# Selective scan: a second of four states by ScalarE products, chunks prepared one chunk earlier, D·x moved into the convolution

## The chip, the cores and the metric

One Trainium2 chip, one core. The metric is the device time of one launch in microseconds (us); lower is better. Engines: PE (TensorE), DVE (VectorE), ACT (ScalarE), POOL (GpSimd), and SP, which here only issues DMAs.

## The reference

Two layers on an image of 256 x 256 tokens with 128 channels, in fp32, each added to its input after a group norm. Layer 0 is a gated attention along rows; the change does not touch it. Layer 1 widens to 256 channels, convolves 3 x 3, and scans the 65,536 tokens in four directions k (row order, column order, and both reversed), with 16 states for each channel:

```
xi, z = split(x @ w_in.T);  z = silu(z);  xc = silu(depthwise_conv3x3(xi))
for each direction k (xs = xc in that order):
    dts, B, C = split(x_proj[k] @ xs)            # 8 + 16 + 16 rows
    delta = softplus(dt_w[k] @ dts + dt_b[k])
    h[t] = exp(delta[t] * A[k]) * h[t-1] + delta[t] * xs[t] * B[t]     # per channel and state
    y_k[t] = sum over states (h[t] * C[t]) + D[k] * xs[t]
out = x + (layernorm(sum_k y_k) * z) @ w_out.T
```

The sum over directions makes the D term of a token (sum of D[k]) * xc.

## The kernel before, in words

Stages one after the other: group norm, attention, convolution (lines 437 to 629), scan (635 to 1173). The convolution goes by blocks of 8 rows, in an order written out by hand: `convolve` (PE), `back` (turns the result to token rows on PE, copies on DVE, and stores xc with one DMA at line 593), `project` (next block; its z goes out by DMA from `zt`, two buffers).

The scan does the directions in the order 2, 1, 3, 0. Each has 128 chunks of T = 512 tokens: 512 chunks q. Of a chunk, the 256 channels are 8 groups g of 32; partition 32j+c of a group holds channel c and, in the free dimension, the states 4j to 4j+3 (i = 0 to 3). So a group is four scans of 128 x 512, and a chunk 32 of them, which I number by slots m = 4g + n, n being the place of the scan in the group's order. The lines:

- `times_B` (875): DVE makes bx[:, :NB] = B_r * ur, for NB = 3 of the four states. B_r holds the rows of B, spread to all partitions by DMA (779); ur is delta*x spread to the group's partitions by a PE product (864). bx has 8 buffers.
- `products` (834), `turn_back` (846): for the fourth state, ACT multiplies delta*x, transposed to token partitions (duT, made by `turn`), by the column of B, 128 columns (four groups) at a time, 32 products a chunk; PE turns the result back by four 128 x 128 transposes a group into bl (PSUM, one buffer).
- The scans (1148): DVE, h = dA*h + bx, in place. dA = exp(delta*A) comes from ACT (1122), into PSUM (three buffers) or, for the state that reads bl, into SBUF (dAl, two buffers). It reads dr, delta spread by DMA (856).
- 1167, 1168: POOL keeps the last column and multiplies the four states by C_r (2048 columns).
- `sums` (890): PE adds up the 16 states with the matrix gather, for four groups (half a chunk) into yp: 32 instructions, emitted in one go at slot 4 of the next chunk and at slot 24. `evacuate` copies yp out on ACT.
- `store` (three directions) adds the running sum yl, loaded by DMA (907), on PE (913, 918), copies it on ACT (940) and stores it; `finish` (the last direction) does the same, then the norm, times z, w_out and the residual.
- `begin_sums` (1073): in the first direction PE starts yp with a product of xs and dg, the diagonal of the summed D.
- `prepare` (721 to 804): from the loaded tokens xs, B, C, delta and du = delta*xs. Softplus is written as max(v,0) + log(1+exp(-|v|)) with a first-order correction: Abs, Relu, Exp, Identity, Identity, Ln on ACT and four POOL operations of 128 x 1024.

The order of all engines' work in the scan is the program's (`manual_schedule`). The loop at line 1103 goes through slots; in each it emits dA, then one piece of each generator that is due (`turning`, `later`, `preparing`, `multiplying`), then the scan, then at fixed n times_B (n = 1), turn_back and spread_du (n = 3). A table `counts` says how many products a slot takes. Engines wait for each other by semaphores, each doing its own list in order. Preparing chunk q+2 begins at slot 21 of chunk q and ends in chunk q+1.

Of the kernel before, what the change touches and what calls it, by code (L numbers as in the profile page):

```python
# [8 lines left out]
F32 = mybir.dt.float32  # L9
# [57 lines left out]
def attention_and_scan_kernel(  # L67
# [35 lines left out]
    y_d = {k: dram.tile([NT, DI], F32, name=f"y{k}_d") for k in (1, 2, 3)}  # L103
# [333 lines left out]
    with tc.tile_pool(name="cw", bufs=1) as cw, tc.tile_pool(name="cs", bufs=2) as cs:  # L437
# [31 lines left out]

        cps = tc.tile_pool(name="cps", bufs=2, space=PSUM)  # L470
# [107 lines left out]
        def back(k, h, xct, xcs):  # L578
# [12 lines left out]
            if h == 1:  # L591
                t0 = RB * k * S
                nc.sync.dma_start(
                    xc_d[t0 : t0 + RB * S, :].rearrange("(c j p) d -> p c j d", p=P, c=4), xct
                )

# [40 lines left out]
    NB = 3  # L637
# [17 lines left out]
    D_s = sw.tile([P, K, 2], F32, name="D_s")  # L655
    nc.scalar.dma_start(D_s, Ds)
    for k in range(1, K):
        nc.vector.tensor_add(D_s[:, 0], D_s[:, 0], D_s[:, k])
    dg = sw.tile([P, 2, P], F32, name="dg")
    for h in range(2):  # L660
        nc.vector.tensor_scalar(dg[:, h, :], ident, D_s[:, 0, h : h + 1], None, ALU.mult)
# [18 lines left out]
    neg_one = sw.tile([P, 1], F32, name="neg_one")  # L680
    nc.vector.memset(neg_one, -1.0)
# [23 lines left out]
    loaded, prepared, summed, turned, products_of = {}, {}, {}, {}, {}  # L705

    def load(q):
        k, a = steps[q]
        xt = io.tile([P, 4, DI], F32, name="xtok", bufs=1)
        src = tokens(xc_d, k, a)  # L710
        n = 4 // len(src)
        for w, s in enumerate(src):
            nc.sync.dma_start(xt[:, n * w : n * w + n, :], s)
        loaded[q] = xt
# [6 lines left out]
    def prepare(q):  # L721
# [13 lines left out]
        yield from until(2, 5)  # L735
# [8 lines left out]
        yield  # L744
        yield
# [4 lines left out]
        yield  # L750


        e = io.tile([P, 2, T], F32, name="e", bufs=1)
        delta = io.tile([P, 2, T], F32, name="delta", bufs=1)
        pvs = []
        for h in range(2):
# [4 lines left out]
            pvs.append(pv)  # L761
        yield
        yield
        for h, pv in enumerate(pvs):
            nc.scalar.activation(e[:, h, :], pv, AF.Abs, bias=dtb_s[:, k, h : h + 1])  # L765
            nc.scalar.activation(delta[:, h, :], pv, AF.Relu, bias=dtb_s[:, k, h : h + 1])
            yield
# [5 lines left out]
        nc.scalar.activation(e, e, AF.Exp, scale=-1.0)  # L773
        B_r = io.tile([P, NB, T], F32, name="B_r")
        C_r = io.tile([P, NI, T], F32, name="C_r")
        for m, t, ni in ((0, B_r, NB), (1, C_r, NI)):
# [6 lines left out]
        yield  # L783
        lg = io.tile([P, 2, T], F32, name="lg", bufs=1)
        nc.scalar.activation(lg, e, AF.Identity, bias=1.0)
        yield
        du = io.tile([P, 2, T], F32, name="du")
        nc.scalar.activation(du, lg, AF.Identity, bias=neg_one)
        B_t = io.tile([P, 4, R + 2 * NS], F32, name="B_t")
        nc.scalar.copy(B_t, tp)  # L790
        yield
        nc.gpsimd.tensor_tensor(e, e, du, ALU.subtract)  # L792
        yield
        yield
        nc.scalar.activation(lg, lg, AF.Ln)  # L795
        yield
        nc.gpsimd.tensor_tensor(lg, lg, e, ALU.add)  # L797
        yield
        nc.gpsimd.tensor_tensor(delta, delta, lg, ALU.add)  # L799
        de_d = sd.tile([DI, T], F32, name="de_d")  # L800
        nc.sync.dma_start(de_d.rearrange("(h p) t -> p h t", p=P), delta)
        yield
        nc.gpsimd.tensor_tensor(du, delta, xs, ALU.mult)  # L803
        prepared[q] = xs, de_d, du, B_r, C_r, B_t

    def turn(q):

        duT = io.tile([P, 4, DI], F32, name="duT", bufs=1)
        turned[q] = duT
        tps = []  # L810
        for w in range(2):
            tp = sps.tile([P, 2, DI], F32, name="tpd", tag="mm")
            for b in range(2):
                for h in range(2):
                    t0 = (2 * w + b) * P
                    nc.tensor.transpose(
                        tp[:, b, h * P : (h + 1) * P], prepared[q][2][:, h, t0 : t0 + P], ident
                    )
            tps.append(tp)
        yield  # L820
        for w, tp in enumerate(tps):
            nc.scalar.copy(duT[:, 2 * w : 2 * w + 2, :], tp)
            yield

    def products(q, h):


        bt = wk.tile([P, 4, 4, 4, 32], F32, name=f"bt{h}", bufs=1)
        products_of[q, h] = bt
        duT, B_t = turned[q], prepared[q][5]  # L830
        for b in range(4):
            for j in range(4):
                n = R + NI * j + NB
                nc.scalar.mul(  # L834
                    bt[:, b, :, j, :],
                    duT[:, b, h * P : (h + 1) * P].rearrange("t (g c) -> t g c", c=32),
                    B_t[:, b, n : n + 1],
                )
                yield

    def turn_back(q, g):

        bl = sps.tile([P, T], F32, name="bl", bufs=1)
        bt = products_of[q, g // 4]
        for b in range(4):
            nc.tensor.transpose(  # L846
                bl[:, b * P : (b + 1) * P], bt[:, b, g % 4].rearrange("t j c -> t (j c)"), ident
            )
        return bl

    def spread_delta(q, h):

        de_d = prepared[q][1]
        dr = io.tile([P, 4, T], F32, name="dr")
        for j in range(4):
            nc.sync.dma_start(
                dr[32 * j : 32 * j + 32],
                de_d[h * P : (h + 1) * P, :].rearrange("(q c) t -> c q t", c=32),
            )
        return dr  # L860

    def spread_du(q, g):
# [4 lines left out]
            prepared[q][2][:, g // 4, :],  # L867
# [5 lines left out]
    def times_B(q, ur):  # L873
        bx = wk.tile([P, NI, T], F32, name="bx", bufs=8)
        nc.vector.tensor_tensor(  # L875
            bx[:, :NB, :],
            prepared[q][3],
# [5 lines left out]
    def sums(q, h):  # L883
# [4 lines left out]
        for i in range(NI):  # L888
            for g, hc in enumerate(his):
# [4 lines left out]
                    start=(i == 0 and steps[q][0] != ORDER[0]),  # L894
# [5 lines left out]
    def load_sum(q):  # L900
# [3 lines left out]
        src = tokens(y_d[ORDER[ORDER.index(k) - 1]], k, a)  # L904
# [5 lines left out]
    def add_sum(ps, yl, blocks):  # L910

        if yl is not None:
            nc.tensor.matmul(ps, ident, yl, start=True, stop=True, skip_group_check=True)  # L913
        for o, yo in blocks:
            if yl is None:
                nc.tensor.transpose(o, yo, ident)
            else:
                nc.tensor.matmul(o, yo, ident, start=False, stop=True, skip_group_check=True)

    def store(q, yos):  # L920
# [3 lines left out]
        yl = summed.pop(q, None)  # L924
        yield
        tps = []
        for h, yo in enumerate(yos):
# [4 lines left out]
                None if yl is None else yl[:, :, hs_],  # L932
# [14 lines left out]
    def finish(q, yos):  # L947
# [25 lines left out]
        zt = io.tile([P, 2, T], F32, name="zl", bufs=1)  # L973
        nc.sync.dma_start(zt, z_d[:, a : a + T].rearrange("(h p) t -> p h t", p=P))
# [11 lines left out]
        yield from until(6, 15)  # L986
        yn = io.tile([P, 4, DI], F32, name="yn", tag="yl", bufs=1)
        for j, now, then in ((0, 15, 16), (1, 16, 19), (2, 19, 20), (3, 20, 27)):
# [7 lines left out]
            yield from until(now, then)  # L996
# [8 lines left out]
        yield from until(27, 31)  # L1005
        gz = io.tile([P, 2, T], F32, name="gz", bufs=1)
# [5 lines left out]
        yield from until(33, 36)  # L1012
# [221 lines left out]
```

## Time and profile before

| what | value |
|---|---|
| median of 3 timed runs (lowest, highest) | 32187.19 us (32186.76, 32198.17) |
| profiled execution, first to last instruction | 32185.1 us, mean PE clock 0.853 |
| busy: PE, DVE, ACT, POOL | 23853.4, 29575.2, 25201.0, 25710.4 us |
| L1148 scans, fed from PSUM dA, from dAl | 12192 at 1264 ns, 4064 at 1254 ns |
| L875 product with B, 128 x 1536 | 4096 at 1727 ns |
| L1122 exp into PSUM, into SBUF | 12288 at 683 ns, 4096 at 713 ns |
| L834 products, 128 x 128 | 16384 at 392 ns |
| L1168 product with C, 128 x 2048 | 4096 at 4542 ns |
| ACT table loads in the scan | 2 a chunk, 1283 ns each |

"L875" is line 875 of the kernel. A row such as `bx<-B_r,ur 128x1536 ... x4096` names what is written and read, the shape and the count. A mean can be longer than the distance from start to start, since instructions of an engine overlap by some 0.1 us. Where the order of time is shown, the columns are start (us), duration (us), engine, line, operation, and in brackets the idle time before it and who ended it.

### The profile page before, as it was taken

The numbers are of one execution on the slowest core, as the hardware profiler recorded it, in microseconds if no ns is written. First come the engines' busy times: TensorE is split into PE (matmuls) and PEld (weight loads), VectorE is DVE, ScalarE is ACT, GpSimd is POOL, SyncE is SP. The second block draws the span as 40 slices with busy tenths as digits, with TensorE's granted clock in tenths as the row PEclk, the third lists the DMA queues.
The fourth block names the chain that finished last, engine by engine and source line by source line (L and its number), as shares of the span: only waits on it lengthen the run. The fifth ranks groups of instructions, "written<-read, shape, count | busy, mean of one in ns | idle before, by whom it ended". The sixth has DMA issues, their size and how long they took to land.

```text
span 32185.1 us, 380702 instructions
## 1 busy us (share of the span) xinstructions
PE 23853.4 (74%) x122902; PEld 10868.3 (34%) x122902; DVE 29575.2 (92%) x29023; ACT 25201.0 (78%) x50438; POOL 25710.4 (80%) x11291
## 2 busy tenths in 40 slices
PE   6999988666676667777777777777777777777777
PEld 3555544222222222222222232223222333333333
DVE  7666633999999999999999999999999999999999
ACT  5555522888888888888888888888888888888888
POOL 4222200999999999999999999999999999999998
PEclk9999999888888888888888888888888888888888
DMA  4001033444444444444444444444444555555554
GB/s 143 30 28 29 27 105 121 110 109 108 111 109 108 110 110 118 119 121 120 119 120 122 119 119 121 121 119 119 122 119 118 123 124 124 123 123 123 124 123 113
DMA packets 2100469, 3518.55 MB, mean 109 GB/s; under 512 B 201112, under 2 KB 1187096, under 8 KB 2022560
## 3 DMA queue, kind: packets, MB, share of 16 engines
q1 hardware_dynamic: 2093296, 3476.09, 43.3%
q8 instruction: 967, 15.84, 0.2%
q10 hardware_dynamic: 5168, 18.12, 0.1%
q14 instruction: 1038, 8.50, 0.1%
HBM read 2754.18 MB, written 739.25 MB: 109 GB/s over the span
## 4 chain that ended last, share of the span: by engine, by line
PE 32%; ACT 24%; DVE 22%; issue 12%; POOL 9%; DMA 2%; SPq 0%; ACTq 0%; POOLq 0%; DVEq 0%
DVE bx L1148 11%; PE yp L890 8%; DVE bx L875 7%; ACT dA L1122 6%; PE ur L864 6%; POOL bx L1168 5%; PE pb L741 3%; ACT bt L834 2%; PE pc L563 2%; ACT dAl L1122 2%; PE av L393 2%; PE tpy L913 2%; POOL at L370 2%; ACT e L765 2%; ACT L795 2%
## 5 line engine op out<-in xcount | busy, mean ns | idle before, releaser
L1168 POOL TENSOR_TENSOR bx<-bx,C_r 128x2048 f32<-128x2048 f32 x4096 | 18604.4, 4542 | 334.3 <-POOL hst L1167 5.8
L1148 DVE TENSOR_TENSOR_SCAN bx<-dA,hst,bx 128x512 f32<-128x512 f32 x12192 | 15074.4, 1264 | 217.2 <-ACT dA L1122 215.3
L1122 ACT ACTIVATE dA<-dr,A_s 128x512 f32<-128x512 f32 x12288 | 8329.3, 683 | 2247.5 <-DVE bx L1148 2199.6
L864 PE MATMUL ur<-du,spread 128*128 128x512 f32 x8192 | 5710.1, 787 | 4498.5 <-DVE bx L875 4378.8
L875 DVE TENSOR_TENSOR bx<-B_r,ur 128x1536 f32<-128x1536 f32 x4096 | 7075.5, 1727 | 40.1 <-DMA dr<-de_d 40.1
L834 ACT ACTIVATE bt<-duT,B_t 128x128 f32<-128x128 f32 x16384 | 5572.5, 392 | 698.7 <-PE bl L846 698.7
L1148 DVE TENSOR_TENSOR_SCAN bx<-dAl,hst,bl 128x512 f32<-128x512 f32 x4064 | 5096.6, 1254 | 24.2 <-PE bl L846 24.1
L890 PE MATMUL yp<-bx,gather 128*32 128x512 f32 x32768 | 5052.5, 771 | 7.5 <-POOL bx L1168 6.4
L846 PE MATMUL bl<-ident,bt 128*128 128x128 f32 x16384 | 2714.8, 289 | 2441.0 <-DVE bx L1148 2439.0
L846 PEld LDWEIGHTS bl<-ident,bt 128*128 128x128 f32 x16384 | 1791.0, 143 | 4323.4 <-DVE bx L1148 3240.7
L864 PEld LDWEIGHTS ur<-du,spread 128*128 128x128 f32 x8192 | 1451.2, 223 | 5027.9 <-DVE bx L875 5023.9
L370 POOL TENSOR_TENSOR at<-at,sm 128x2048 f32<-128x2048 f32 x256 | 922.2, 3603 | 2719.7 <-DVE sm L369 2550.6
L1122 ACT ACTIVATE dAl<-dr,A_s 128x512 f32<-128x512 f32 x4096 | 2919.2, 713 | 0.0
L890 PEld LDWEIGHTS yp<-bx,gather 128*32 128x32 f32 x32768 | 1165.1, 139 | 4348.3 <-issue 3834.9
L1167 POOL COPY hst<-bx 128x4 f32<-128x4 f32 x4096 | 771.4, 188 | 1615.5 <-DVE bx L1148 1588.6
L362 ACT ACTIVATE at<-at,mx 128x256 f32<-128x256 f32 x2048 | 1016.1, 498 | 472.5 <-DVE mx L358 468.1
L792 POOL TENSOR_TENSOR e<-e,du 128x1024 f32<-128x1024 f32 x512 | 1202.8, 2349 | 138.3 <-DMA C_r<-bc_d 138.3
L799 POOL TENSOR_TENSOR delta<-delta,lg 128x1024 f32<-128x1024 f32 x512 | 1209.9, 2363 | 40.1
L803 POOL TENSOR_TENSOR du<-delta,xs 128x1024 f32<-128x1024 f32 x512 | 1205.4, 2354 | 40.2
L758 PE MATMUL pv<-bc,dtw_s 8*128 8x512 f32 x2048 | 1019.6, 616 | 256.5 <-ACT bc L747 256.5
L797 POOL TENSOR_TENSOR lg<-lg,e 128x1024 f32<-128x1024 f32 x512 | 1205.0, 2354 | 0.2 <-ACT lg L795 0.2
L391 DVE COPY aT<-atp 128x512 f32<-128x512 f32 x512 | 353.6, 691 | 774.8 <-PE atp L382 771.0
(173 smaller groups left out, 31933.7 us busy)
## 6 DMA issues: line engine op xcount, KB each, us to landing
dr<-de_d SPq DMA_DIRECT2D x4096, 256.0 KB
C_r<-bc_d SPq DMA_DIRECT2D x2048, 256.0 KB
B_r<-bc_d SPq DMA_DIRECT2D x2048, 192.0 KB
de_d<-delta SPq DMA_DIRECT2D x512, 512.0 KB
xtok<-xc_d SPq DMA_DIRECT2D x256, 512.0 KB
xtok<-xc_d SPq DMA_DIRECT2D x512, 256.0 KB
yl<-y_d SPq DMA_DIRECT2D x512, 256.0 KB
y_d<-yt SPq DMA_DIRECT2D x512, 256.0 KB
```

Of the source, the lines that this page charges most:

```text
L370: nc.gpsimd.tensor_tensor(at, at, sm.unsqueeze(3).to_broadcast([P, H, 2, S]), ALU.mult,)
L797: nc.gpsimd.tensor_tensor(lg, lg, e, ALU.add)
L799: nc.gpsimd.tensor_tensor(delta, delta, lg, ALU.add)
L803: nc.gpsimd.tensor_tensor(du, delta, xs, ALU.mult)
L834: nc.scalar.mul(bt[:, b, :, j, :], duT[:, b, h * P : (h + 1) * P].rearrange("t (g c) -> t g c", c=32), B_t[:, b, n : n + 1],)
L846: nc.tensor.transpose(bl[:, b * P : (b + 1) * P], bt[:, b, g % 4].rearrange("t j c -> t (j c)"), ident)
L864: nc.tensor.matmul(ur, spread[:, g % 4].rearrange("p j c -> p (j c)"), prepared[q][2][:, g // 4, :], start=True, stop=True,)
L875: nc.vector.tensor_tensor(bx[:, :NB, :], prepared[q][3], ur.unsqueeze(1).to_broadcast([P, NB, T]), ALU.mult,)
L890: nc.tensor.matmul(yp[32 * g : 32 * g + 32, :], gather, hc[:, i, :], start=(i == 0 and steps[q][0] != ORDER[0]), stop=True, skip_group_che ...
L1122: nc.scalar.activation(dA, dr, AF.Exp, scale=A_s[:, k, g // 4, g % 4, i : i + 1])
L1148: nc.vector.tensor_tensor_scan(hs[:, i, :], dA, hs[:, i, :] if i < NB else bls.pop((q, g)), 0.0 if a == 0 else hst[:, g, i : i + 1], ALU.mult,
L1168: nc.gpsimd.tensor_tensor(hs, hs, prepared[q][4], ALU.mult)
```

## The change

- NB goes from 3 to 2: two states of four come by ACT products. A product now takes all 8 groups, 256 columns; there are still 32 a chunk, one in every slot, into bt2 and bt3 with two buffers each, made a whole chunk ahead. turn_back runs twice a group, at n = 1 and n = 3, into bl2 and bl3 (one PSUM buffer each). The order of states in a group is 2, 0, 3, 1. dA in PSUM has two buffers instead of three.
- bx has 7 buffers instead of 8.
- `prepare(q+2)` starts at slot 6 of chunk q and ends in the same chunk, with duT in it; delta is one Softplus activation for each half; du overwrites xs. B_r and C_r of chunk q+1 are loaded from slot 10 of chunk q on (`replicate`).
- dr is loaded by group, two groups ahead, with three buffers.
- `sums` goes out in quarters, one a slot: slots 5 to 8 (for the chunk before) and 21 to 24. `store` and `finish` start at slot 20 and have new distances between their pieces.
- D*xc is made in the convolution on POOL from the block that is stored, and stored to its own array by a DMA; the first direction loads it as its running sum, as the others load theirs. begin_sums loses its product.

The diff, cut:

```diff
-    y_d = {k: dram.tile([NT, DI], F32, name=f"y{k}_d") for k in (1, 2, 3)}
+    y_d = {k: dram.tile([NT, DI], F32, name=f"y{k}_d") for k in (1, 2, 3, K)}
...
+                xd = cs.tile([P, 4, 4, DI], F32, name="xd", bufs=1)
+                nc.gpsimd.tensor_tensor(
+                    xd.rearrange("p c j d -> p (c j) d"),
+                    xct.rearrange("p c j d -> p (c j) d"),
+                    D_row.unsqueeze(1).to_broadcast([P, 16, DI]),
+                    ALU.mult,
+                )
+                nc.sync.dma_start(
+                    y_d[K][t0 : t0 + RB * S, :].rearrange("(c j p) d -> p c j d", p=P, c=4), xd
                 )
...
-    NB = 3
+    NB = 2
...
+        for h, pv in enumerate(pvs):
+            nc.scalar.activation(
+                delta[:, h, :], pv, AF.Softplus, bias=dtb_s[:, k, h : h + 1]
+            )
+        de_d = sd.tile([DI, T], F32, name="de_d", bufs=3)
+        nc.sync.dma_start(de_d.rearrange("(h p) t -> p h t", p=P), delta)
         yield
...
+        nc.gpsimd.tensor_tensor(xs, delta, xs, ALU.mult)
...
+    def products(q):
+        duT, B_t = prepared[q][2], prepared[q][4]
+        products_of[q] = []
+        for i in range(NB, NI):
+            bt = wk.tile([P, 4, NG, 4, 32], F32, name=f"bt{i}")
+            products_of[q].append(bt)
+            for b in range(4):
+                for j in range(4):
+                    n = R + NI * j + i
+                    nc.scalar.mul(
+                        bt[:, b, :, j, :],
+                        duT[:, b, :].rearrange("t (g c) -> t g c", c=32),
+                        B_t[:, b, n : n + 1],
+                    )
+                    yield
+
+    def turn_back(q, g, i):
+        bl = sps.tile([P, T], F32, name=f"bl{i}", bufs=1)
+        bt = products_of[q][i]
...
+    def spread_delta(q, g):
+        dr = io.tile([P, T], F32, name="dr", bufs=3)
+        nc.sync.dma_start(
+            dr, prepared[q][1][32 * g : 32 * g + 32, :].unsqueeze(0).to_broadcast([4, 32, T])
+        )
...
-        bx = wk.tile([P, NI, T], F32, name="bx", bufs=8)
+        bx = wk.tile([P, NI, T], F32, name="bx", bufs=7)
...
+        zt = io.tile([P, 2, T], F32, name="zl", tag="yl", bufs=1)
+        nc.sync.dma_start(zt, z_d[:, a : a + T].rearrange("(h p) t -> p h t", p=P))
...
-        for n, i in enumerate((NB, *range(NB))):
+        for n, i in enumerate((NB, 0, NB + 1, 1)):
             if i < NB:
-                dA = sps.tile([P, T], F32, name="dA", bufs=3)
+                dA = sps.tile([P, T], F32, name="dA", bufs=2)
...
+            if n == 0 and g == 0 and q + 1 < NQ:
+                multiplying.append(products(q + 1))
+            if n == 1 and g == 0 and q + 2 < NQ:
+                load(q + 2)
+            if n == 2 and g == 1 and q + 2 < NQ:
+                preparing.append(prepare(q + 2))
+            if n == 2 and g == 2 and q + 1 < NQ:
+                replicating.append(replicate(q + 1))
...
+            if n == 1 and g == 1 and q:
+                summing.append(sums(q - 1, 1))
+            if n == 1 and g == 5:
+                summing.append(sums(q, 0))
+            if n == 0 and g == 5 and finishing:
+                later.append(finishing.pop())
             pieces(later)
             piece(preparing)
-            for _ in range(counts[g][n] if g in counts else 0):
-                piece(multiplying)
+            piece(replicating)
+            piece(multiplying)
+            piece(summing)
...
             if n == 1 and nxt:
                 bxs[nxt] = times_B(nxt[0], urs.pop(nxt))
-            if n == 3 and nxt:
-                bls[nxt] = turn_back(*nxt)
+            if n % 2 and nxt:
+                bls[(*nxt, n // 2)] = turn_back(*nxt, n // 2)
             if n == 3 and s + 2 < len(all_steps):
                 urs[all_steps[s + 2]] = spread_du(*all_steps[s + 2])
```

## The prediction

> **What bounds the kernel now.** I read the page's slices first, then busy time by stage, then the order of time on VectorE (DVE) and TensorE (PE) inside one chunk. The stages (PE, PE weight loads, DVE, ScalarE/ACT, GpSimd/POOL, then clock, DMA share):
>
> ```profile
> 4200.00:5400.00 1200.00, 1143.47 (x18383) 599.52 (x18381) 387.49 (x565) 272.06 (x453) 17.85 (x42) 1.00 0.37 123
> 12180.00:18660.00 6480.00, 4613.65 (x20266) 1900.17 (x20264) 6454.34 (x5066) 5497.97 (x10636) 5933.89 (x2532) 0.83 0.49 120
> 25340.00:32100.00 6760.00, 4966.00 (x23308) 2389.93 (x23306) 6598.11 (x6020) 5879.15 (x11405) 6375.07 (x3134) 0.83 0.51 123
> ```
>
> The scan runs from 5590 us to the end, 512 chunks. In it DVE is busy 6454 of 6480 us (99.6%), and in the last direction 97.6%: DVE is the bound. One group of a chunk on DVE, in order of time:
>
> ```profile
> 15003.25 1.72 DVE L875 TENSOR_TENSOR bx<-B_r,ur 128x1536 f32<-128x1536 f32 x1
> 15004.89 2.45 DVE L1148 TENSOR_TENSOR_SCAN bx<-dA,hst,bx 128x512 f32<-128x512 f32 x2
> 15007.26 1.25 DVE L1148 TENSOR_TENSOR_SCAN bx<-dAl,hst,bl 128x512 f32<-128x512 f32 x1
> 15008.43 1.25 DVE L1148 TENSOR_TENSOR_SCAN bx<-dA,hst,bx 128x512 f32<-128x512 f32 x1
> 15009.61 1.72 DVE L875 TENSOR_TENSOR bx<-B_r,ur 128x1536 f32<-128x1536 f32 x1
> ```
>
> Start to start, a scan takes 1.175 us, the product with B 1.64, a group 6.36; eight are 50.9, and chunks follow every 51.2 us. PE in the same chunk:
>
> ```profile
> 15011.39 1.71 PE L864 MATMUL ur<-du,spread 128*128 128x512 f32 x2 [2.16 <-DVE bx L875]
> 15013.03 4.70 PE L890 MATMUL yp<-bx,gather 128*32 128x512 f32 x32
> 15017.65 0.66 PE L846 MATMUL bl<-ident,bt 128*128 128x128 f32 x4
> 15018.15 1.02 PE L864 MATMUL ur<-du,spread 128*128 128x512 f32 x2
> 15024.42 2.08 PE L864 MATMUL ur<-du,spread 128*128 128x512 f32 x2 [2.48 <-DVE bx L875]
> 15026.86 2.05 PE L913 MATMUL tpy<-yl,ident 128*128 128x512 f32 x2 [0.36 <-DMA yl<-y_d]
> ```
>
> See two things. PE waits for DVE, often over 2 us, so its bursts (4.70 us of yp) are covered. And the same ur takes 1.02 us in a busy stretch, about 2.0 after a wait: the clock records say 0.5 or 1.0, 0.83 on average.
>
> **What the Trainium skill says.** "ScalarE: Activation LUTs", section "What ACT_TABLE_LOAD costs": 0.833 ns a column, pointer operands extra, and 1283 ns for a table load. The trace agrees: bt at 128 columns 392 ns, dAl at 512 columns 713, loads 1283. "TensorE: Matmul & The Clock Gate", Part 1: an activity monitor halves the clock in free windows of 3.4 us. The trace agrees: its clock records come in multiples of 3.413 us. Matched with PE's busy share in the scan stage, a window under 0.39 was nearly always followed by half clock; full clock held from 0.43 up, and half clock ended only after 0.8 or more. Same page, Part 2: matmuls keep program order; the order of time above shows it.
>
> **The change, part by part.** Slot m = 4g+n of a chunk, T(m) the end of its scan.
>
> *DVE.* The product falls from 1536 to 1024 columns. L401 (512 columns, 692 ns) and L875 (1536, 1727 ns) give 1.01 ns a column, so 0.52 us off 1.64. A group is 5.84, a chunk 46.7 instead of 50.9. That is 4096 x 0.52 = 2130 us, if DVE stays the bound. Both kinds of scan cost the same (1264 and 1254 ns).
>
> *ACT.* Busy now 5498/6480 x 51.2 = 43.4 us a chunk. 32 products at 256 instead of 128 columns add 32 x 0.107 = 3.4 (estimate from the ScalarE page's slope; the trace's bt to dAl slope is 0.836). Abs, Relu, Exp, two Identity, Ln go (4 x 0.57 + 0.95 + 0.95 + 1.04 + 1.06 = 6.3 start to start), two Softplus come: no row and no page shows one, the ScalarE page finds functions equal per column, so I take the Abs price, 0.57 each; the ends are no table load (2.6 us less than now) and four loads (2.6 more). I keep two. Net -1.5: 41.9 of 46.7, still covered. The Softplus burst (2 x 1.28 + 2 x 0.57 = 3.7) lies under four slots of lead, 5.8 us.
>
> *POOL* loses three of four 2.36 us operations, 46.9 to 39.8 us a chunk. *DMA* loses a third of B_r and gains 512 KB a chunk in the first direction: even. dr becomes eight issues, each three buffers ahead, a window of two groups, 11.7 us: covered; on SP it stands behind bc_d, de_d and y_d stores, which wait for ACT work that ACT does anyway before it frees the dr buffer. Loading and preparing a whole chunk earlier moves their DMAs (xtok, bc_d, B_r, C_r, de_d) on SP, with free buffers when they come up: cost 0. In the last direction zl now shares yl's buffer and waits on SP until PE has done tpz; dr for slot 12 stands behind it, about 2 us late of 11.7: 0.
>
> *D·x* in the convolution: two L1168 prices a block, 32 x 9.1 = 290 us on a POOL busy 18 of 1200 us, plus 64 MB written at DMA share 0.37. PE bounds that stage. SP queues z_d stores and the next row loads behind the 9 us wait; zt has two buffers and a pair of units every 20 us. Cost 0; exposed 290. Start-up: chunk 1 is prepared ahead of the first scan and 32 products precede it, +30 us (estimate from the 54 us it takes now).
>
> *PE, where the stall comes from.* bl doubles: 8 more groups at 0.5 us, 36.4 to about 40 us of a shorter chunk; the dg product of the first direction goes, an L913 pair comes in its place. The order matters more. turn_back at slot 19 waits for T(18), since bl3 has one buffer, and all of the following queues behind it: bl3 0.6, ur 1.0, tpy 1.75 (L913 0.86, L918 0.89), sums 0.9 (a quarter of yp at full clock, 8 instructions), bl2 0.6, tpy 1.75, sums 0.9, sums 0.9, bl3 0.6, ur 1.0, sums 0.9, gaps and hand-over 0.3: done at T(18)+11.2. The last sums piece (slot 24) frees the bx buffer that times_B at slot 25 needs, because 7 buffers put group 7 on group 0's. DVE gets there after 7 scans and a product, T(18)+9.3. Stall 1.9 at full clock. Before, 8 buffers and sums drained at group 6 left a whole group of room. Same figure at slots 3 to 9: bl3, ur, four sums, two tps, bl2, bl3, ur end at T(2)+8.45 against 9.3: 0.9 to spare.
>
> Half clock: in light groups PE does bl2, then bl3 and ur, so most windows lie under 0.4 and the clock halves; it returns after one window filled by the burst, 3 to 6.6 us in. That makes the first part (bl3, ur, L913: 2.5 us) about 4.9: +2.35. At slot 5 two to three light groups precede: always, stall 2.35-0.9 = 1.4. At slot 19 about 8 in 10 window positions, shorter: +1.4. With yl landing late and small rest 0.3: 1.9+1.4+1.4+0.3 = 5.0 us a chunk, against 4.2 gained and 0.3 to 1.4 of present stalls removed. ACT and POOL are ahead by then.
>
> Sum: first scan 5590 + 30; 512 x 46.72 = 23,921; norm statistics 128 x 1.57 = 201; stalls 512 x 5.0 = 2560; tail 51: **32,353, say 32,350**. The same sum for before gives 5590 + 26,051 + 201 + 298 (stalls 0.3, and 1.4 in the last direction) + 51 = 32,191 against a span of 32,185.1; the median of the timed runs is 32,187.2.
>
> **Rivals.**
> (B) *The light groups keep the full clock, and only queue length costs.* For: more PE work in every group, a second bl shortens idle stretches. Against: windows holding one bl are still 20% busy. Stall 1.9 + 0.2: 29,793 + 512 x 2.15 = 30,900. It decides if the stall is under 4.6 us a chunk: this is the rival on the faster side.
> (C) *The PE backlog compounds:* tpy waits for yl (issue to landing about 10 us, issued behind ACT's slot 15), the yt copies then hold ACT at slot 25, dA comes late. For: L913 shows waits on the yl DMA already. Against: 14.7 us in total now. 7.0 us a chunk: 33,380.
> (D) Softplus or D·x doesn't do what it says: bounded above at 2.6 us a chunk less and 290 us more; within the range.
>
> **Chances.** My forecast 0.50 (its own range 32,000 to 32,700), B 0.28, C 0.22. Range 30,800 to 33,400. About 0.2% is what a measurement here can tell from no change (32,121 to 32,249). Of my forecast a quarter lies below that and 0.13 within: faster 0.28 + 0.12 = 0.40, same 0.07, slower 0.53.
>
> **What would show it.** Right: the product at 1.1 us start to start; DVE idle before the product with B at groups 2 and 6, released by PE yp; chunks every 51 to 52 us; PE's clock still near 0.83; ACT idle mostly on PE or DVE. B: clock over 0.93 in the scan, chunks near 49. C: DVE waits on ACT dA after yt. Wrong altogether: DVE idle before scans for bl or dr, or POOL releasing yp last.

## The result, and the profile after

The changed kernel takes **32188.24 us** (median of 12 runs, 32177.96 to 32199.31), the kernel before on the same chip 32186.88 us (12 runs). The ratio is 1.000, with a 95% interval of 0.9992 to 1.0009: no difference. I had forecast 32,350 us, slower by 0.5%; the time lies in the range, but the direction that I gave the most chance did not come.

The profiled execution spans 32186.4 us, against 32185.1 before. The same three stages, with the same columns as above (length; PE, PE weight loads, DVE, ACT, POOL; clock, DMA share, GB/s):

```profile
4200.00:5400.00 1200.00, 1149.96 (x18543) 611.23 (x18513) 388.72 (x566) 272.87 (x454) 258.89 (x68) 0.99 0.51 171
12180.00:18660.00 6480.00, 5115.82 (x24291) 2437.91 (x24292) 5916.36 (x5056) 5360.75 (x9863) 5058.63 (x2150) 0.83 0.44 115
25340.00:32100.00 6760.00, 5419.43 (x27443) 2818.91 (x27436) 6132.07 (x6053) 5657.34 (x10693) 5543.45 (x2772) 0.87 0.44 119
```

In the scan DVE falls from 6454 to 5916 us of 6480, so 538 us of work have gone from this stretch, and yet as many instructions (5056 after, 5066 before) pass in it. DVE now stands idle for 8.7% of it. The clock is 0.83, as before. Who ends that idle time is in the view of waits by engine (in all, times, longest, all in us but the times):

```profile
DVE bx L872 <- PE yp L887: 2165.4, 913, 3.8
...
DVE bx L1129 <- ACT dA L1101: 102.4, 196, 4.4
```

913 waits in 512 chunks are nearly two a chunk; L872 is times_B, L887 the sums. In the order of time on DVE, around the longer of the two (slots 23 to 26, then the other wait, at slot 9 of the next chunk):

```profile
15012.42 1.25 DVE L1129 TENSOR_TENSOR_SCAN bx<-dAl,hst,bl 128x512 f32<-128x512 f32 x1
15013.59 1.26 DVE L1129 TENSOR_TENSOR_SCAN bx<-dA,hst,bx 128x512 f32<-128x512 f32 x1
15018.18 1.22 DVE L872 TENSOR_TENSOR bx<-B_r,ur 128x1024 f32<-128x1024 f32 x1 [3.34 <-PE yp L887]
15019.32 1.27 DVE L1129 TENSOR_TENSOR_SCAN bx<-dAl,hst,bl 128x512 f32<-128x512 f32 x1
...
15042.64 1.22 DVE L872 TENSOR_TENSOR bx<-B_r,ur 128x1024 f32<-128x1024 f32 x1 [1.05 <-PE yp L887]
```

And what PE was doing meanwhile:

```profile
15005.65 1.09 PE L846 MATMUL bl<-ident,bt 128*128 128x128 f32 x4 [1.60 <-DVE bx L1129]
15006.53 1.92 PE L861 MATMUL ur<-xs,spread 128*128 128x512 f32 x2
15008.23 1.34 PE L909 MATMUL tpy<-yl,ident 128*128 128x512 f32 x2
15009.41 1.05 PE L911 MATMUL tpy<-ident,yo 128*128 128x128 f32 x8
15010.39 1.07 PE L887 MATMUL yp<-bx,gather 128*32 128x512 f32 x8
15011.39 0.66 PE L846 MATMUL bl<-ident,bt 128*128 128x128 f32 x4
15011.88 1.02 PE L909 MATMUL tpy<-yl,ident 128*128 128x512 f32 x2
15012.74 1.05 PE L911 MATMUL tpy<-ident,yo 128*128 128x128 f32 x8
15013.73 1.92 PE L887 MATMUL yp<-bx,gather 128*32 128x512 f32 x16
15015.58 0.66 PE L846 MATMUL bl<-ident,bt 128*128 128x128 f32 x4
15016.07 1.02 PE L861 MATMUL ur<-xs,spread 128*128 128x512 f32 x2
15017.03 1.07 PE L887 MATMUL yp<-bx,gather 128*32 128x512 f32 x8
```

PE waits for a scan, starts bl3, and then works without a gap for 12.4 us. The first ur takes 1.92 us and the later one 1.02: the burst starts at half clock. Its last quarter of the sums ends at 15018.1, and DVE, which stopped at 15014.8, starts the product at 15018.18. This is the queue that the prediction laid out, in its order.

Summed by group (from one product with B to the next, mean of a direction, worked out from the trace; work is 5.82 us a group):

| | before | after, first direction | after, last direction |
|---|---|---|---|
| plain group | 6.36 | 5.82 | 5.82 |
| group 2 (slot 9) | 6.67 | 7.00 | 5.97 |
| group 6 (slot 25) | 6.36 | 9.26 | 10.42 |
| chunk | 51.20 | 51.26 | 53.60 |

In the first three directions after, each chunk has 1.17 us of wait at slot 9 and 3.43 at slot 25: 4.6 us, against 4.3 saved on eight products. These are means; most chunks take 51.20 us, as before, and some take more. In the last direction the waits come to 5.4 us, with 1.57 us of norm statistics in group 7. The chunks before took 51.20, 51.19, 51.18 and 53.88 us by direction.

### The profile page after: what moved, and what is told of

Its sections match the earlier page's. It is cut to its first block, busy times and chain, and to the rows that moved or that the text cites. A ratio compares the mean times of both kernels' runs of the same rounds, so it can differ in the third digit from the quotient of the medians.

```text
span 32186.4 us, 417546 instructions
## 1 busy us (share of the span) xinstructions
PE 25927.0 (81%) x140314; PEld 13062.6 (41%) x140314; DVE 27464.9 (85%) x29024; ACT 24568.8 (76%) x47363; POOL 22480.8 (70%) x9787
## 4 chain that ended last, share of the span: by engine, by line
PE 49%; DVE 29%; issue 10%; ACT 5%; DMA 3%; POOL 3%; SPq 0%; POOLq 0%; ACTq 0%; DVEq 0%
DVE bx L1129 18%; PE yp L887 13%; PE ur L861 9%; PE bl L846 8%; DVE bx L872 7%; DMA yl<-y_d 2%; PE tpy L909 2%; PE tpy L911 2%; PE pc L575 2%; PE av L393 2%; POOL at L370 2%; ACT bt L834 2%; PE atp L382 2%; PE tps L743 1%; DVE at L357 1%
## 5 line engine op out<-in xcount | busy, mean ns | idle before, releaser
L846 PE MATMUL bl<-ident,bt 128*128 128x128 f32 x32768 | 6314.9, 324 | 5392.8 <-DVE bx L1129 5392.1
L1129 DVE TENSOR_TENSOR_SCAN bx<-dAl,hst,bl 128x512 f32<-128x512 f32 x8128 | 10276.7, 1264 | 121.6 <-ACT dA L1101 78.3
L1129 DVE TENSOR_TENSOR_SCAN bx<-dA,hst,bx 128x512 f32<-128x512 f32 x8128 | 10223.1, 1258 | 23.5 <-ACT dA L1101 23.5
L846 PEld LDWEIGHTS bl<-ident,bt 128*128 128x128 f32 x32768 | 4260.6, 163 | 11474.0 <-issue 5939.9
L834 ACT ACTIVATE bt<-duT,B_t 128x256 f32<-128x256 f32 x16384 | 8223.2, 502 | 0.0
L872 DVE TENSOR_TENSOR bx<-B_r,ur 128x1024 f32<-128x1024 f32 x4096 | 4922.1, 1202 | 2233.1 <-PE yp L887 2165.4
L1101 ACT ACTIVATE dAl<-dr,A_s 128x512 f32<-128x512 f32 x8192 | 5861.3, 715 | 971.4 <-DVE bx L1129 923.7
L861 PE MATMUL ur<-xs,spread 128*128 128x512 f32 x8192 | 5812.2, 801 | 5.0 <-DVE bx L872 5.0
L1101 ACT ACTIVATE dA<-dr,A_s 128x512 f32<-128x512 f32 x8192 | 5587.5, 682 | 85.4 <-DVE bx L1129 3.2
L887 PE MATMUL yp<-bx,gather 128*32 128x512 f32 x32768 | 4520.8, 637 | 5.7 <-POOL bx L1144 4.2
L861 PEld LDWEIGHTS ur<-xs,spread 128*128 128x128 f32 x8192 | 1663.6, 252 | 6.6 <-DVE bx L872 6.6
L887 PEld LDWEIGHTS yp<-bx,gather 128*32 128x32 f32 x32768 | 716.8, 111 | 2072.4 <-issue 1796.5
## 6 DMA issues: line engine op xcount, KB each, us to landing
dr<-de_d SPq DMA_DIRECT2D x4096, 256.0 KB
C_r<-bc_d SPq DMA_DIRECT2D x2048, 256.0 KB
xtok<-xc_d SPq DMA_DIRECT2D x512, 256.0 KB
yl<-y_d SPq DMA_DIRECT2D x512, 256.0 KB
```

The source lines that it names most:

```text
L834: nc.scalar.mul(bt[:, b, :, j, :], duT[:, b, :].rearrange("t (g c) -> t g c", c=32), B_t[:, b, n : n + 1],)
L846: nc.tensor.transpose(bl[:, b * P : (b + 1) * P], bt[:, b, g].rearrange("t j c -> t (j c)"), ident)
L861: nc.tensor.matmul(ur, spread[:, g % 4].rearrange("p j c -> p (j c)"), prepared[q][0][:, g // 4, :], start=True, stop=True,)
L872: nc.vector.tensor_tensor(bx[:, :NB, :], replicas[q][0], ur.unsqueeze(1).to_broadcast([P, NB, T]), ALU.mult,)
L887: nc.tensor.matmul(yp[32 * g : 32 * g + 32, :], gather, hc[:, i, :], start=(i == 0), stop=True, skip_group_check=True,)
L1101: nc.scalar.activation(dA, dr, AF.Exp, scale=A_s[:, k, g // 4, g % 4, i : i + 1])
```

## The experiments

The theory that came out of the result, the **queue theory**: the 4.6 us are PE's program order (bl3, ur, tpy and sums in one queue) and its half clock at the start of the burst. The rivals were another wait behind it that holds the chunk above 49 us anyway, and the seven buffers of bx by themselves. Ratios are to the kernel before on the same chip; the edits are to the kernel after unless said otherwise. The four directions' chunk times, as means worked out from the trace, are given as 47.7 x3 / 50.9 for three and the last; a window is the 3.413 us in which the clock records come.

**1. Sums of one state.** It leaves three of four states out of the output.

```diff
-        for i in range(NI):
+        for i in range(1):
```

> The kernel after, but sums adds up only state 0 of four (the output leaves out the other three). This takes 12 of 16 sums products a half chunk off TensorE. Theory Q (the TensorE queue between slots 19 and 25 and between 3 and 9, in program order, is what VectorE waits for): 2.7 us less work in each stretch, so both waits go, chunks of 46.7 to 47.5 us instead of 51.2, total 29,800 to 30,300 us. Rival R (seven bx buffers alone: the product with B waits for the release in slot 24, whatever stands in the queue): the release still comes in slot 21 now, so it predicts about the same as Q here. Rival A (ScalarE or the DMAs are a second bound hidden behind the waits): chunks stay above 49 us.

Measured: 30486 us, 0.9472 (0.9453 to 0.9491); chunks 47.7 x3 / 50.9. The wait on the sums is gone; some waits on ur and bl stay:

```profile
DVE bx L872 <- PE ur L861: 264.9, 469, 1.1
...
DVE bx L1129 <- PE bl L846: 184.2, 64, 5.3
```

The time is a little above what the queue theory expected, but nothing holds the chunk above 49 us: that rival falls.

**2. A full clock.** PE makes the transposes of bl2 four times at slots 1, 13, 17 and 29: extra work, so that fewer windows count as light.

```diff
-        for b in range(4):
+        for b in [b for _ in range(times) for b in range(4)]:
...
+                bls[(*nxt, n // 2)] = turn_back(
+                    *nxt, n // 2, 4 if n == 1 and g in (0, 3, 4, 7) else 1
+                )
```

> The kernel after, with the four transposes of turn_back at slots 1, 13, 17 and 29 done four times over (the same result). It adds 1.5 us of TensorE work four times a chunk, where TensorE waits for VectorE by more than 2.5 us, so that no clock window falls under a 0.4 busy share. Theory Q with the half clock as part of the wait: the wait at slot 9 goes, the one at slot 25 falls from 3.4 to about 1.9 us, chunks of 48.5 us, mean clock above 0.95, total about 30,900 us. Rival (the clock is beside the point and only the amount of TensorE work counts): 6 us more TensorE work, chunks of 51.2 us or more, total 32,190 or above.

Measured: 31228.6 us, 0.9703 (0.9687 to 0.972); chunks 49.0 x3 / 52.9. The second stage above, and the wait:

```profile
12180.00:18660.00 6480.00, 5224.95 (x31742) 2810.75 (x31740) 6180.94 (x5286) 5584.05 (x10313) 5305.28 (x2247) 1.00 0.45 120
```

```profile
DVE bx L872 <- PE yp L887: 1259.3, 506, 3.9
```

7451 more matmuls than after (48 repeats a chunk, and more chunks in the stretch) cost PE only 109 us more, because the clock is 1.00 and not 0.83. Waits fall from 913 to 506, one a chunk: slot 9 has none, slot 25 still about 2.2 us. So some 2.3 of the 4.6 us were the half clock, and the rest is the queue's length. It fell short of the expected 30,900 since I had put slot 25 at full clock lower, at 1.9.

**3. The store later.** In three directions the running sum starts at slot 27, after the burst.

```diff
-            if n == 0 and g == 5 and finishing:
+            if finishing and (g, n) == ((5, 0) if steps[q - 1][0] == ORDER[-1] else (6, 3)):
```

> The kernel after, with store (three of four directions) started at slot 27 instead of 20, so that its two tpy pieces no longer stand among the sums pieces. The last direction is left as it is. Theory Q: 3.5 us less in the queue between slots 19 and 25, the wait at slot 25 goes or stays under 0.7 us, the one at slot 9 stays near 1.1 or shrinks; chunks of 46.9 to 48 us in three directions, total 30,600 to 31,000 us. Rival R (the seven buffers alone): the release stays in slot 24, so the wait at slot 25 stays over 2 us, total 32,000 us or more.

Measured: 31038.9 us, 0.9643 (0.9629 to 0.9658); chunks 48.28 x3 / 53.5, a little above what the queue theory expected. In three directions slot 25 waits 0.3 us, slot 9 still 0.9; in all:

```profile
DVE bx L872 <- PE yp L887: 894.3, 590, 3.9
```

bx has seven buffers here too, so the buffers alone are not the cause: it is what PE has to do before it frees one.

**4. The sums one slot earlier.**

```diff
-            if n == 1 and g == 1 and q:
+            if n == 0 and g == 1 and q:
...
-            if n == 1 and g == 5:
+            if n == 0 and g == 5:
```

> The kernel after, with the four sums pieces one slot earlier (4 to 7 and 20 to 23). The last one then stands ahead of bl and ur in TensorE's order and frees the bx buffer about 1.5 to 2 us earlier, while the work that TensorE has until ur for group 7 is the same. Theory Q: the wait at slot 25 stays within 1 us of 3.4, now released by ur; total 31,900 to 32,300 us. Rival R: the wait at slot 25 falls to 1.5 us, total about 31,200 us.

Measured: 32087.5 us, 0.997 (0.9958 to 0.9982); chunks 51.2 x3 / 52.9. The buffer comes free sooner, and at slot 25 the wait has another name and the same length, 3.5 us (in the order of time at 15,000 us 2.6 on ur and 0.7 on dA just before it):

```profile
DVE bx L872 <- PE ur L861: 1723.5, 934, 2.7
```

ur stands in the same queue, now behind the sums. Freeing the buffer early buys nothing while the whole burst must pass first: again the queue, and not the buffers (whose rival expected 31,200). This experiment is weaker than 3: its chunks lie at 15 windows again, and experiments 13 and 14 show that there a saving can be filled up by a wait.

**5. Both 2 and 3.**

> The kernel after with both edits: the repeated transposes at slots 1, 13, 17 and 29, and store started at slot 27. Theory Q: what the clock costs and what the length of the queue costs are parts of the same wait, so both together leave VectorE nearly without one in three directions: chunks of 46.7 to 47.3 us there, 52.8 in the last direction as with the repeated transposes alone, total 30,350 to 30,600 us. Rival (a second bound lies just below, on ScalarE or in the DMAs): three-direction chunks stay at 48 us or more, total 30,900 or more.

Measured: 30979.3 us, 0.9625 (0.9609 to 0.9641), clock 0.988; chunks 48.27 x3 / 53.1. This missed the expected 30,350 to 30,600, and the rival's numbers came. A new wait took the place of the old ones, at group 0:

```profile
DVE bx L1129 <- PE bl L846: 562.7, 389, 4.2
```

By the order of time, ACT's copy of yp (slot 30) now stands 2.7 us until PE has read the old yo; the copies of duT behind it free a PSUM buffer late, the store's second tpy waits for that buffer on PE (1.2 us), and bl for the next chunk, here made four times over, stands behind it. In experiment 8 this copy goes out one slot later, and the wait is gone: it was the order again, not a second bound.

**6 and 7. More work on DVE, as copies.** Does the chunk give way when DVE has more to do? Four copies of 128 x 128 at slot 29 of after (the edit shown), two in the kernel before.

```diff
+            if g == 7 and n == 1:
+                for _ in range(4):
+                    nc.vector.tensor_copy(extra, ident)
```

> The kernel after, with four small VectorE copies (128 x 128) more in each chunk, at slot 29, where VectorE doesn't wait; about 0.6 to 0.8 us of VectorE work a chunk. Theory L (the chunk is locked to 15 windows of the TensorE clock, 15 x 3.413 = 51.20 us: the wait shrinks when VectorE's own work grows, since it depends on where the windows lie): median chunk stays at 51.20 us in three directions, total 32,180 to 32,300 us. Rival S (wait and work simply add): chunks of 51.8 to 52.0 us, total 32,500 to 32,600 us.

> The kernel before, with two small VectorE copies (128 x 128) more in each chunk at slot 29, 0.3 to 0.4 us of VectorE work. Before, a chunk is 50.88 us of VectorE work and a wait of 0.31 us for ScalarE, together 51.20 as well. Theory L for the kernel before too: median chunk stays at 51.20 to 51.25 us, total within 30 us of the kernel before. Rival S (the equality of the two chunk times is a coincidence): 51.5 to 51.6 us, total 32,330 to 32,400 us.

Measured: 34476.6 us, 1.0712 (1.0696 to 1.0728), and 33731.8 us, 1.0481 (1.0466 to 1.0497). The test says nothing of the lock, for a reason of its own; the lines are of experiment 6:

```profile
15035.08 4.50 POOL L1148 TENSOR_TENSOR bx<-bx,C_r 128x2048 f32<-128x2048 f32 x1
...
15035.83 4.62 DVE L1132 COPY extra<-ident 128x128 f32<-128x128 f32 x4
...
15040.36 1.28 DVE L1133 TENSOR_TENSOR_SCAN bx<-dA,hst,bx 128x512 f32<-128x512 f32 x1
```

The first copy ends when POOL's product ends (15039.6), 3.8 us after its start; each of the others takes 0.23 us. The Trainium skill has this under "SBUF — State Buffer", section "Who interferes with whom": DVE copies that use the port pair shared with GpSimd block against it for a whole instruction. The trace agrees.

**8. The best version.** Experiment 5, with the finish of the last direction later too: it starts at slot 27, its yl is loaded at slot 20, the w_out piece moves a slot forward, and the first half of yp is copied at slot 31.

```diff
-        yield from until(22, 31)
+        yield from until(22, 30)
...
-        if g == 4 and q:
+        if g == (5 if steps[q - 1][0] == ORDER[-1] else 4) and q:
...
-            if n == 2 and g == 7:
+            if n == 3 and g == 7:
...
-            if n == 0 and g == 5 and finishing:
+            if finishing and (g, n) == (6, 3):
```

> e5_both, and the last direction treated alike: finish starts at slot 27, its running sum is loaded at slot 20, its po pieces stand at slot 25, and yp of the first half is copied out at slot 31. Theory Q: the wait of 4 us at slot 25 of the last direction goes too, chunks of 48.3 to 50 us there (46.7 and 1.6 of norm statistics), total 29,800 to 30,150 us. Rival (in the last direction ScalarE's heavier list is the bound): no better than e5_both there, total 30,400 us or more.

Measured: **30178.3 us, 0.9377 (0.9363 to 0.939)**, the fastest; chunks 46.84 x3 / 51.24. Second stage:

```profile
12180.00:18660.00 6480.00, 5392.70 (x33210) 2941.72 (x33210) 6470.92 (x5536) 5790.10 (x10794) 5555.87 (x2354) 1.00 0.47 126
```

DVE is busy 6471 of 6480 us: without the stalls, all of the 4.3 us a chunk arrive. The last direction keeps some 3 us of waits at groups 0 and 2, more than expected, so the total lies just above the 30,150 us.

**9 and 10. More work on DVE, as bn_stats,** an operation that the trace shows unhindered beside POOL's product: three of them at slot 29 of after, two in the kernel before. By the order of time they cost 0.85 and 0.53 us a chunk, more than I had expected. The rival to plain adding up was by now that the chunk is locked to PE's clock windows: 51.20 us is 15 windows of 3.413.

```diff
+            if g == 7 and n == 1:
+                for _ in range(3):
+                    nc.vector.bn_stats(extra, ident)
```

> The lock tried again without the copies, some of which took 3.9 us: the kernel after with three bn_stats of 128 x 128 more in each chunk at slot 29, about 0.55 us of VectorE work. Theory L (the chunk is held at 15 clock windows, 51.20 us): median chunk 51.20 us in three directions, total within 60 us of the kernel after. Rival S (wait and work add): 51.75 us, total about 32,460 us.

> The kernel before with two bn_stats of 128 x 128 more in each chunk at slot 29, about 0.35 us of VectorE work. Theory L for the kernel before: its wait of 0.31 us for ScalarE gives way, chunks of 51.20 to 51.25 us, total within 40 us of the kernel before. Rival S: 51.55 us, total about 32,350 us.

Measured: 32777.3 us, 1.018 (1.0163 to 1.0197), and 32305.7 us, 1.0038 (1.0023 to 1.0053). After passes the work on: chunks of 52.12 us as median and 52.36 as mean, since three of 51.86, 53.04 and 52.12 us come round again and again. That is 1.1 us for 0.85 of work. In the kernel before the chunk becomes 51.41 us (median), just its DVE work (8 x 6.36 + 0.53), and its wait of 0.31 us on dA is gone; that lies between the two expectations. There is no lock against growth.

**11. Experiment 8 without the repeated transposes.**

> The fastest version so far (store and finish from slot 27, yp copied out at slot 31) without the repeated transposes. Theory Q: with the queue short the half clock costs less; its share of the wait comes back only at slot 9 (up to 1.4 us) and little at slot 25: chunks of 47.3 to 48.3 us in three directions against 46.84 with the repeated transposes, total 30,350 to 30,800 us. Rival (the repeats do nothing once the queue is short): 46.84 us again, total 30,180 us.

Measured: 30753.3 us, 0.9555 (0.9541 to 0.9569), clock 0.88; chunks 47.79 x3 / 52.9. The wait at slot 9 is back, with 1.1 us. So the clock is worth 0.95 us a chunk even with the short queue. And 47.79 us is 14.00 windows.

**12. Softplus alone, in the kernel before.** Abs, Relu, Exp, two Identity, Ln and three POOL operations give way to two Softplus; nothing else changes. The diff, cut:

```diff
-            nc.scalar.activation(e[:, h, :], pv, AF.Abs, bias=dtb_s[:, k, h : h + 1])
-            nc.scalar.activation(delta[:, h, :], pv, AF.Relu, bias=dtb_s[:, k, h : h + 1])
+            nc.scalar.activation(delta[:, h, :], pv, AF.Softplus, bias=dtb_s[:, k, h : h + 1])
```

> One part alone: the kernel before with delta made by two Softplus activations, as in the kernel after, and without the six ScalarE and three GpSimd operations that they replace (places in the order unchanged). Theory: VectorE is the bound, so this is off the path; at most the wait of 0.31 us for ScalarE at group 2 goes, chunks of 50.9 to 51.2 us, total 32,020 to 32,190 us. Rival (Softplus brings more table loads, or the freed ScalarE and GpSimd time counts): over 32,250 us, or under 31,900 us.

Measured: 31950.0 us, 0.9927 (0.9912 to 0.9942). The second stage (ACT busy 4917 us, 5498 before):

```profile
12180.00:18660.00 6480.00, 4747.63 (x20328) 2023.86 (x20320) 6462.65 (x5081) 4917.03 (x9906) 5089.73 (x2160) 0.80 0.49 120
```

One part of the change gains 0.7% by itself: the wait on dA goes, and the last direction falls from 53.88 to 52.81 us, which takes the total below what I had expected. The chunk of the other three is 50.88 us as median, just the work of DVE. That this gain is lost in the whole change because DVE waits longer for PE there is argued, and not shown.

**13 and 14. Less work on DVE.** One scan of 32 goes over 256 of its 512 columns, 0.53 us less a chunk, in both kernels (half of that scan's result is left out). If the waits were plain queue lengths, the kernel after would gain 0.53 us a chunk, some 270 us: its cut, at slot 31, lies outside of both stretches in which DVE waits for PE (slots 19 to 25 and 3 to 9). If the chunk is held from below at 15 windows, nothing happens.

```diff
+            w = 256 if (g, n) == (7, 3) else T
             nc.vector.tensor_tensor_scan(
-                hs[:, i, :],
-                dA,
+                hs[:, i, :w],
+                dA[:, :w],
```

> The kernel after, with the scan at slot 31 run over 256 of its 512 columns (it leaves out half of one of 32 scans a chunk), so 0.53 us less VectorE work, at a place without a wait. Theory H (a chunk is held from below: where its work and its least wait come to a little under 15 clock windows, the chunk slides along the windows until the wait fills it up): median chunk still 51.20 us in three directions, total within 60 us of the kernel after in these. Rival S (wait and work add, the equality is a coincidence): 50.67 us, total about 31,920 us.

> The kernel before with the same cut (the scan at slot 31 over 256 of 512 columns). Theory H: its wait for ScalarE grows from 0.31 to about 0.85 us and the chunk stays at 51.20 us, total within 60 us of the kernel before. Rival S: 50.67 us with the wait unchanged, or 50.35 us without it; total 31,760 to 31,920 us.

Measured: 32162.1 us, 0.999 (0.9983 to 0.9997), and 32190.4 us, 0.9999 (0.999 to 1.0008). As means, chunks stay at 51.20 x3 in both.

In experiment 13 the single chunks do not: the median is 50.88, and not the 51.20 that I had expected. Five chunks come round again and again, 50.74, 50.88, 51.87, 50.74 and 51.78 us, together 256.0 us or 75 windows. The waits for yp are fewer than the 913 of the kernel after, and longer:

```profile
DVE bx L872 <- PE yp L887: 2133.5, 683, 3.9
```

Set beside the clock records of the same trace, the waits follow the half clock. In three of the five chunks PE has none between slots 2 and 9, and slot 9 does not wait; between slots 18 and 25 it has 5.5 to 6.2 us, and the wait up to slot 25 is 4.5 to 4.8 us. In the other two it has 5.7 to 5.9 us in the first stretch (wait 2.1 to 2.2) and 3.4 in the second (wait 3.5). Over all chunks of three directions, a microsecond more of half clock between slots 18 and 25 goes with 0.46 us more wait (0.49 in the kernel after). By the means, the cut moved half clock out of the stretch that has 0.9 us to spare (3.5 to 2.3 us) into the one that has nothing to spare (3.4 to 4.85 us), where the wait grew from 3.43 to about 4.2 us.

In experiment 14 the wait on dA grew by what was cut; first the kernel before, then the experiment, at the same slot (9):

```profile
15021.44 1.28 DVE L1148 TENSOR_TENSOR_SCAN bx<-dA,hst,bx 128x512 f32<-128x512 f32 x1 [0.20 <-ACT dA L1122]
```

```profile
15025.23 1.28 DVE L1149 TENSOR_TENSOR_SCAN bx<-dA,hst,bx 128x512 f32<-128x512 f32 x1 [0.74 <-ACT dA L1122]
```

Waits there last 217.3 us in all before, 476.0 in the experiment. This wait ends a path that leaves DVE at its product after slot 21. These lines of the kernel before are of the next chunk's path, which starts with the product at 15041.72:

```profile
15043.50 2.08 PE L864 MATMUL ur<-du,spread 128*128 128x512 f32 x2 [2.16 <-DVE bx L875]
15045.51 5.52 PE L890 MATMUL yp<-bx,gather 128*32 128x512 f32 x32
...
15052.40 1.91 PE L741 MATMUL pb<-xs,xw_in 128*40 128x512 f32 x4
15054.35 0.58 ACT L747 COPY bc<-pb 40x512 f32<-40x512 f32 x1 [0.91 <-PE pb L741]
```

PE works through ur, yp, bl, ur and pb, ACT then through its own list without a gap, up to the dA for slot 9. From the product to the scan at slot 9 this takes 30.92 us in the kernel before and in experiment 14 alike, 12.6 of them up to ACT's copy of pb (PE's part). Slot 31 lies inside this path, so the cut alone could not have shortened it, whatever the clock does. But the path has no fixed length. After the first change of direction the kernel before runs four chunks of 50.88 us without a wait; PE's part then mostly takes 11.4 to 11.5 us, with 3.41 us of half clock in it. Then a second half-clock window falls into it (6.83 us), PE's part grows to 12.25 and on to 12.63, and within some ten chunks the chunk settles at 51.20. Experiment 14 does the same, from a chunk of 50.35 us. So the clock holds the kernel before as well, through PE's part of this path. Half a microsecond of work taken away from the busiest engine changes nothing: both kernels are held.

## Why the prediction was right or wrong

Its own sum against the trace after:

| term | predicted | measured |
|---|---|---|
| first scan starts | 5590 + 30 | 5601.9 |
| DVE work of a chunk | 46.72 | 46.6 |
| wait at slot 9 | 1.4 | 1.17 |
| wait at slot 25 | 1.9 + 1.4 | 3.43 |
| yl late, small rest | 0.3 | about 0 |
| waits, all directions | 5.0 | 4.8 (4.6 x3, 5.4) |
| last scan to end | 51 | 54.0 |

The sum then ends 18 + 512 x (0.12 + 0.18) - 3 = 169 us lower: 32,353 - 169 = 32,184, against the span of 32,186.4.

**Right:** where the gain goes. The product takes 1.12 us start to start, DVE's work fell as worked out, and the two waits stand at slots 9 and 25, released by yp, with the clock at 0.83. Experiments 1, 2, 3, 8 and 11 show both causes: the queue's length (1, 3) and the half clock (2, 11). Rival B (full clock kept, chunks near 49) and rival C (a growing backlog, ACT late) did not come: the clock is 0.83, and waits on dA come to 102 us in all.

The covered edits were covered. The Softplus takes 683 ns on the trace with two table loads a chunk at 1283 ns, as taken; the product on ACT 502 ns, estimated 499. (The sum for ACT has a slip without consequence: 3.4 - 6.3 + 1.1 is -1.8, not -1.5. ACT is busy 42.4 us a chunk after.) D·x cost 32 operations of 8.9 us on POOL, hidden: the scan's first product with B starts at 5577.6 us instead of 5576.2. These lines are of the kernel after (busy, mean ns; idle before):

```profile
L834 ACT ACTIVATE bt<-duT,B_t 128x256 f32<-128x256 f32 x16384 | 8223.2, 502 | 0.0
...
L773 ACT ACTIVATE delta<-pv,dtb_s 128x512 f32<-128x512 f32 x1024 | 647.8, 683 | 9.4 <-PE pv L767 3.2
...
L609 POOL TENSOR_TENSOR xd<-xct,D_row 128x4096 f32<-128x4096 f32 x32 | 284.6, 8894 | 793.8 <-DVE xct L598 793.8
```

**Wrong:** the step "1.9+1.4+1.4+0.3 = 5.0 us a chunk, against 4.2 gained". The mechanism was right; the term for the stalls was too large. In three directions they measure 4.6 us: the 0.3 for a late yl and a rest was not there, slot 9 waits 1.17 and not 1.4, slot 25 3.43 and not 3.3. Over all directions the stalls are 4.8, and the work of DVE is 46.6 and not 46.72. Since gain and loss are both over 4 us, these 0.3 us of 51 decided the sign. I gave no change only 0.07, as the sum of two independent sizes.

What I had not seen is that they are not independent. I read the kernel before as bound by DVE, with PE's bursts covered; but there too a path through PE's burst sets the chunk (experiment 14). The clock records of both kernels repeat every 51.2 us, 15 windows. By experiments 13 and 14 taking a little more work off DVE does not shorten such a chunk: half clock moves into the path through PE until the chunk, or a round of five, fills whole windows. Experiments 9 and 10 show that a longer chunk does become longer. A chunk that DVE alone sets is not held: 50.88 us in experiment 12. This is why most chunks of both kernels take 51.20 us: before, 50.9 us of work and a wait on ACT; after, 46.6 and two waits on PE. That the totals agree to 0.01% is luck on top of it: in the means, three directions are 26 us longer after, the last one is 36 us shorter, and the start and the end add 15.

**What stays open.** That the hold needs the changing clock is read from the traces, and fits the experiments at full clock, whose chunks are no whole number of windows (49.0 us are 14.4, 46.84 are 13.7). The kernel before with a full clock was not tried. Nor is every kernel with waits on PE at changing clock held: experiment 3, with a clock of 0.89, has chunks of 48.28 us, 14.1 windows, and why was not followed.

## What to carry to other kernels

When work is taken off the busiest engine, list what another engine does in program order between the same two points, at the clock that it will have there: here 4.3 us saved met 11 to 12 us of PE work in a stretch that DVE now crosses in 9.3. Spread that burst, keep PE's windows full, and the saving arrives (46.84 us a chunk, 6.2% in all); without the change of order the removed work was worth nothing. And test a period that looks like a multiple of 3.413 us by a small cut on the busiest engine: if the time doesn't move, the largest busy share isn't the bound. Then follow the path that ends at the wait: a cut that lies inside it is lost in any case, and tells nothing of the clock.

## What the runs showed of the hardware that was not expected

- A loop with PE at changing clock on its longest path can be held at a whole number of clock windows: 51.20 us (15) in both kernels and in experiment 14, 47.79 (14) in experiment 11, and five chunks together at 75 in experiment 13.
- More PE work made the kernel faster: 48 repeated transposes a chunk raised the clock in the scan from 0.83 to 1.00 and took 3% off (experiment 2).
- A DVE copy of 128 x 128 went from 0.23 to 3.8 us behind a GpSimd product; bn_stats of the same tile did not wait.
